# A graph-network kernel whose scatters each get a permission of their own, and a different order of its first steps

## The chip, the cores and the metric

The kernel runs as one program on one core of a Trainium2 chip. A core has a matrix engine (TensorE, PE in the profile, with its weight loads as PEld), a vector engine (VectorE, DVE), a scalar engine (ScalarE, ACT), a general engine (GpSimd, POOL), and a sync engine (SyncE, SP) that here only issues DMAs. Each engine runs its own list of instructions in order, and they meet through semaphores. The metric is the time of one execution on the device, in microseconds.

## The reference

One layer of message passing on a graph with N = 12500 nodes of 128 features and E = 412500 edges with 20 edge features each. Edges are sorted by `dst`; `src` is in no order.

```python
h0  = relu(layernorm(x))                          # 12500 x 128
h   = h0 @ W_in2f                                 # one row a node
Wij = ssp(f @ W_f1 + b_f1) @ W_f2 + b_f2          # one row an edge, from 20 features
Wij = Wij * rcut[:, None]                         # ssp(x) = softplus(x) - log 2
agg = segment_sum(h[dst] * Wij, src, N)           # sum over the edges of a node
out = x + ssp(agg @ W_o1 + b_o1) @ W_o2 + b_o2
```

## The kernel before

**Chunks and steps.** The edges are cut into 806 chunks of 512 (`NCH`), a chunk into four tiles of 128 (`QT`). A long Python loop writes the program out step by step; `step(k)` puts the work for chunk k and for chunks some steps ahead into the engines' lists, and this order is the order in which each engine runs it. In the steady part a step holds:

- `message(k)`: VectorE multiplies the edge's filter row by the row of h that it needs, o = v * hg (L864), and chunk k is put on the list `waiting` of chunks to be scattered.
- `picked` for chunk k+1: ScalarE scales the picked rows of h by `rcut`, four times, into `hg` (L856).
- `value` for chunk k+1: TensorE multiplies the softplus outputs by W_f2 onto a bias that ScalarE wrote earlier, eight matmuls (L834). The last one is kept as `kept["v"]`.
- `pick` for chunk k+2: TensorE takes rows of h from a small window `near` with a one-hot matrix `at` (L846).
- `window`, `end`, `blocks`, `compare`: VectorE's comparisons and the end of softplus for later chunks (L742, L747, L932).
- `rank` and `rank_end` for chunk k+6: two matmuls (L799 `rest_of`, L766 `after`) keep count of how many edges each block of 128 nodes has had, and VectorE's reduction (L771) reads from that the place at which each edge's row will be stored.
- `hidden` for chunk k+4, for two chunks at a time: z = f @ W_f1 (L710), with the exponential and the logarithm on ScalarE in between (L719 to L722).
- `add`: TensorE sums rows of an earlier part of the edges, one unit (L953).

**Scatter and sums.** The products o are not summed at once. Each tile of 128 rows is written by an indirect DMA to a table `slots` in device memory, into a slot of the block that its `src` lies in. These 3224 scatters (four a chunk, L873) all sit in GpSimd's queue. The edges form seven segments (`SEGS`); segment 0 is chunks 0 to 351. When a segment is complete, its table is read back block by block and summed by matmuls with one-hot matrices, beside the chunks of the next segment. These sums begin `DELAY` = 17 steps after the end of a segment, so the first begin in step 369, and they go on until the end.

**What a scatter waits for.** The tile of o (VectorE) and the DMA that used the same of eight semaphores before (the eighth scatter back). Beside these there is an added wait, which orders nothing that the data need: from chunk 24 (`PACED`) until shortly before the end, the first of the four scatters of chunk k-1 (`LAG` = 1) waits for the last v matmul of step k. So GpSimd cannot run ahead of TensorE's step. TensorE in its turn waits in `behind` for the scatters of chunk k-16 (`BACK`), as o has 16 buffers.

**The start.** The nodes come in quads of 512. `make_h` is a generator that makes h for one quad in pieces: load x, layer-norm statistics on VectorE, normalisation, transposes (L367) on TensorE, product with W_in2f (L373), splitting into three bf16 parts, stores to the tables that `near` is loaded from. The first quad, `h[0]`, is done ahead of step -3. The second, `h[1]`, is advanced by one piece within step 0 and by one after each step from 0 on. `HEAD` = (0, 2, 4) are steps whose log and end of softplus stand in other places than usual. For `0 <= k < HEAD[-1]`, that is in steps 0 to 3, the message of chunk k+1 comes in step k, ahead of its counts, and not at the head of step k+1.

Of the kernel before, what the change touches and what calls it, by code (L numbers as in the profile page):

```python
# [17 lines left out]
P = 128  # L18
# [3 lines left out]
QT = CH // P  # L22
# [23 lines left out]
def gnn_kernel(  # L46
# [20 lines left out]
    nc = tc.nc  # L67
# [477 lines left out]
    with tc.tile_pool(name="edge", bufs=2) as edge, tc.tile_pool(  # L545
# [49 lines left out]
        def behind(inst, k, i):  # L595

            if k - BACK >= 0:
                tc.add_manual_dep(inst.ins, puts[(k - BACK) * QT + i],
                                  mybir.DependencyInfo(mybir.DependencyClass.Sync,
                                                       mybir.DependencyReason.DATA),  # L600
                                  reason="pace of the scatters")

        class Group:
# [101 lines left out]
            def hidden(self, c):  # L705

                z = psum.tile([P, 2, CH], F32, name="z")
                for k in range(2):
                    rows = slice(32 * (c + k), 32 * (c + k) + RBF)
                    mm = nc.tensor.matmul(z[:, k, :], wf1[rows, :], self.f[rows, :],  # L710
                                          start=True, stop=True)
                    if k == 1:
                        behind(mm, self.g * NCHUNK + c - LZ, 3)
                self.pair[c] = z

            def hidden_log(self, c):
# [36 lines left out]
            def rank(self, c):  # L753

                seg = self.seg
                if c == 0:
                    self.top = edge.tile([P, TG], F32, name="top")
                    self.slot = edge.tile([P, TG], I32, name="slot", bufs=8)
                k = self.g * NCHUNK + c
                if k > seg.c0:  # L760
                    self.pass_on()
                if k == seg.cleared and k > seg.c0:
                    used = self.used()
                    self.limit(6 * len(segs), ALU.is_gt, seg.low, used[:, :, :NBLK - 1])
                    self.limit(6 * len(segs) + 1, ALU.is_gt, seg.low_last, used[:, :, NBLK - 1:])
                nc.tensor.matmul(free, after, self.inb[c], start=k == seg.c0, stop=False,  # L766
                                 skip_group_check=True)
                kept["inb"] = self.inb[c]

            def rank_end(self, c):  # L770
# [58 lines left out]
            def value(self, c, v):  # L829

                r = self.pair[c // 2 * 2][:, c % 2, :]
                k = self.g * NCHUNK + c - 1
                for i in range(QT):
                    mm = nc.tensor.matmul(v[:, i, :], r[:, i * P:(i + 1) * P], wf2,  # L834
                                          start=False, stop=True, skip_group_check=True)
                    if i == 1:
                        behind(mm, k, k % 2)
                kept["v"] = mm
                return v

            def pick(self, c, at, ps):

                near = self.near.pop(c)
                k = self.g * NCHUNK + c - 2
                for i in range(QT):
                    mm = nc.tensor.matmul(ps[:, i, :], at[:, i * P:(i + 1) * P], near,  # L846
                                          start=i == 0, stop=i == QT - 1, skip_group_check=True)
                    if i == 1:
                        behind(mm, k, 2 + k % 2)

            def picked(self, c, ps):

# [11 lines left out]
                nc.vector.tensor_mul(o[:, :, :P], v, hg)  # L864
                self.o[c] = o

            def scatter(self, c, after=None):

                views = self.seg.views
                o = self.o.pop(c)  # L870
                for i in range(QT):
                    j = c * QT + i
                    put = nc.gpsimd.indirect_dma_start(  # L873
                        out=views[j % VIEWS],
                        out_offset=bass.IndirectOffsetOnAxis(ap=self.slot[:, j:j + 1], axis=0),
                        in_=o[:, i, :],
                        in_offset=None,
                    )
                    puts.append(put.ins.name)
                    if i == 0 and after is not None:  # L880
                        tc.add_manual_dep(
                            put.ins, after.ins.name,
                            mybir.DependencyInfo(mybir.DependencyClass.Sync,
                                                 mybir.DependencyReason.DATA),
                            reason="pace of TensorE")
                    if i == 0 and self.g * NCHUNK + c == self.seg.cleared:
                        for name in self.seg.clears:
                            tc.add_manual_dep(
                                put.ins, name,
                                mybir.DependencyInfo(mybir.DependencyClass.Sync,  # L890
                                                     mybir.DependencyReason.DATA),
                                reason="cleared slots")

        class Collect:
# [47 lines left out]
            def add(self, u):  # L942
                b0, nb, t0, nt = self.units[u]
                m, to = self.m.pop(u), self.to.pop(u)
                for j in range(nb * nt):
                    b, t = b0 + j // nt, t0 + j % nt
                    if b % QT == 0 and t == 0:
                        self.few = QT if "rest" in kept else 2
                    few = self.few
                    i = b % few  # L950
                    if i == 0 and t == 0:
                        self.acc[b // few] = self.room(b // few)
                    nc.tensor.matmul(self.acc[b // few][:, i, :], m[:, j, :P], to[:, j, :],  # L953
                                     start=t == 0, stop=t == self.seg.tiles(b) - 1)
                    if t == self.seg.tiles(b) - 1 and (i == few - 1 or b == NBLK - 1):
                        self.done.append((b, few))
                        owed.append(self)
# [39 lines left out]
        def of(k):  # L997
            return groups[k // NCHUNK], k % NCHUNK
# [14 lines left out]
        def pairs(make):  # L1013
            return lambda g, c: None if c % 2 else make(g, c)
# [34 lines left out]
        tops, ps = [], {}  # L1049
        waiting = []  # L1050
        LAG, PACED = 1, 24

        def step(k, units=()):

# [11 lines left out]
            def message(k):  # L1066
                g, c = of(k)
                g.message(c, vs.pop(k), hgs.pop(k))
                waiting.append(k)
                scatter(k)  # L1070

            def scatter(k, after=None):
                while waiting and (waiting[0] < PACED or k >= NCH - PACED // 2
                                   or after is not None and waiting[0] <= k - LAG):
                    j = waiting.pop(0)
                    g, c = of(j)
                    g.scatter(c, after if j >= PACED and k < NCH - PACED // 2 else None)

            if k in vs:
                message(k)  # L1080
            if not k:
                next(h[1])
            for r in tops:
                for _ in r:
                    pass
# [8 lines left out]
            if has(k + 1):  # L1094
                g, c = of(k + 1)
                hgs[k + 1] = g.picked(c, ps.pop(k + 1))
                if k + 1 not in vs:
                    vs[k + 1] = g.value(c, bs.pop(k + 1))
                    scatter(k, kept["v"])
            if k in HEAD:  # L1100
                part("log", k + LZ - 1, pairs(hidden_log))
            if has(k + 2):
                g, c = of(k + 2)
                if k + 2 not in ps:
                    ps[k + 2] = psum.tile([P, QT, P], F32, name="picked", tag="v", bufs=3)
                g.pick(c, ats.pop(k + 2), ps[k + 2])
                if k + 2 > 0:
                    bs[k + 2] = g.bias(c)
            part("window", k + 3, window)
            if k not in HEAD:  # L1110
                part("end", min(k + LZ - 2, made.get("log", -1)), pairs(hidden_end))
# [4 lines left out]
                    keep()  # L1116
            if k < NCH:
                keep()
            if 0 <= k < HEAD[-1]:
                message(k + 1)  # L1120
            upto = max(made["rank"], min(k + LR, 2 * k + 3))
            ready = [ranks(j) for j in range(made["rank"] + 1, upto + 1)]
# [4 lines left out]
            for r in ready[-1:]:  # L1127
                next(r, None)
                tops.append(r)
            if k in HEAD:  # L1130
                part("end", made["log"] - 1, pairs(hidden_end))
            elif k != -1:
                part("log", min(k + LZ - 1, made["hidden"]), pairs(hidden_log))
            if k not in HEAD[:-1]:
                part("hidden", k + LZ, pairs(hidden))
            for c, u in units:
                if summed:
                    summed[0].add(summed[1])
                summed[:] = c, u

        zeros = {}
        units = {}
# [129 lines left out]
        with tc.manual_schedule():  # L1272
# [36 lines left out]
            for k in range(-3, max(NCH, max(units) + 1)):  # L1309
# [9 lines left out]
                step(k, now)  # L1319

                if k >= 0:
                    for m in h:
                        next(m, None)
                if k > NEXT - 3:
                    next(aside, None)
# [124 lines left out]
```

## Time and profile before

| | |
|---|---|
| time, median of 3 runs | 5023.69 us (5019.35 to 5025.19) |
| profiled execution, its own time | 5066.41 us |
| its span from the first instruction to the last | 5064.7 us |
| mean granted TensorE clock | 0.784 of full speed |
| busy: TensorE matmul, weight load | 3601.4 us (71%), 2760.7 us (55%) |
| busy: VectorE, ScalarE, GpSimd | 3149.0 us (62%), 2793.9 us (55%), 3135.5 us (62%) |
| DMA | 858.10 MB, 169 GB/s on the mean |

How to read the lines that follow. In the table of stretches a row gives the stretch's start and end, its length, and for each engine the busy microseconds and, in brackets, the number of instructions; then the granted clock (PEclk), the share of DMA time and the rate. In the groups, a row reads: line, engine, operation, output <- inputs, x count, then busy time and the mean nanoseconds of one, then the engine's idle time just before these instructions and what ended it. A line of the waits gives the waiting group, what it waited for, the total idle time and how often. In a timeline, a row gives the start, the duration, engine, line, operation, and in square brackets the idle time ahead with the instruction that ended it; "issue" means that the profile shows nothing that it waited for.

### The profile page before, as it was taken

Reading aid. Unit: us, or ns where it says so; the run is one execution under the profiler, and the core shown is the slowest. Engines: PE = TensorE matmul, PEld = TensorE weight load, DVE = VectorE, ACT = ScalarE, POOL = GpSimd, SP = SyncE. Lnnn points to the kernel's source line nnn. Section 1 sums busy time; section 2 is a strip of 40 time slices with the busy share of each in tenths; the row PEclk is TensorE's granted clock in tenths of the full one; section 3 lists DMA queues with packets and bytes.
Section 4 is the critical chain, followed back from the end, with each engine's and each line's share of the span. In section 5 each row is a group of like instructions: output and inputs, shape, how many; then the busy total and the mean of one; then the engine's idle time right before and its main releaser. Section 6 shows DMA issues by size and latency. Waiting matters only on the chain. (4 is left out here: it accounts for less than half of the span.)

```text
span 5064.7 us, 68387 instructions
## 1 busy us (share of the span) xinstructions
PE 3601.4 (71%) x21594; PEld 2760.7 (55%) x21594; DVE 3149.0 (62%) x7192; ACT 2793.9 (55%) x5494; POOL 3135.5 (62%) x3298
## 2 busy tenths in 40 slices
PE   5666666566655565567777887887777787787778
PEld 3444444344433344356666666666666666666667
DVE  5565555555544454556666666666666676677767
ACT  5556566565555555555555555555555555555533
POOL 5566666666666666666666666666656666666553
PEclk7666666766666666679999888888988888888889
DMA  4555545445433334446657655567656765665658
GB/s 140 171 160 164 171 138 174 147 134 160 130 99 114 113 113 141 131 154 199 190 189 238 187 178 185 175 192 230 188 169 185 219 207 168 183 216 163 186 144 229
DMA packets 494767, 858.10 MB, mean 169 GB/s; under 512 B 141018, under 2 KB 276558, under 8 KB 494398
## 3 DMA queue, kind: packets, MB, share of 16 engines
q1 hardware_dynamic: 390798, 640.38, 42.3%
q0 software_dynamic: 103168, 213.15, 12.5%
q8 instruction: 174, 2.85, 0.2%
q14 instruction: 195, 1.60, 0.1%
q10 hardware_dynamic: 432, 0.13, 0.0%
HBM read 457.62 MB, written 395.69 MB: 168 GB/s over the span
## 5 line engine op out<-in xcount | busy, mean ns | idle before, releaser
L873 POOL DMA_INDIRECT slots<-o,slot x3224 | 3090.8, 959 | 1831.2 <-issue 808.9
L856 ACT ACTIVATE hg<-picked,rcut 128x128 f32<-128x128 f32 x3224 | 913.3, 366 | 1243.5 <-remote 356.7
L834 PEld LDWEIGHTS v<-wf,r 128*128 128x128 f32 x6448 | 1067.2, 247 | 324.2 <-issue 214.8
L834 PE MATMUL v<-wf,r 128*128 128x128 f32 x6448 | 1153.8, 335 | 73.4 <-issue 36.5
L864 DVE TENSOR_TENSOR o<-v,hg 128x512 f32<-128x512 f32 x806 | 553.0, 686 | 698.4 <-remote 207.0
L953 PEld LDWEIGHTS acc<-to,m 128*128 128x128 f32 x5660 | 782.1, 219 | 281.0 <-issue 144.0
L953 PE MATMUL acc<-to,m 128*128 128x128 f32 x5660 | 836.6, 308 | 117.1 <-DVE agg L987 45.2
L710 PE MATMUL z<-f,wf 20*128 20x512 f32 x1612 | 605.7, 826 | 355.7 <-issue 185.6
L771 DVE TENSOR_REDUCE top<-free 128x4 f32<-128x392 f32 x806 | 449.1, 557 | 602.2 <-remote 341.9
L932 DVE TENSOR_TENSOR to<-numbers,m 128x640 f32<-128x640 f32 (+3 forms) x793 | 630.4, 825 | 40.0 <-remote 12.0
L719 ACT ACTIVATE a<-z,bf 128x1024 f32<-128x1024 f32 x402 | 445.7, 1109 | 379.4 <-PE v L834 113.6
L747 DVE TENSOR_TENSOR inb<-numbers,blk 128x392 f16<-128x392 f32 x806 | 447.7, 556 | 297.3 <-PE picked L846 73.9
L846 PE MATMUL picked<-near,at 126*128 126x128 bf16 x3224 | 393.6, 248 | 330.2 <-issue 193.5
L799 PE MATMUL free<-inb,rest_of 128*128 128x392 f16 x806 | 318.1, 395 | 420.9 <-issue 277.2
L742 DVE SCALAR_TENSOR_TENSOR r<-z,nbf,a 128x1024 f32<-128x1024 f32 x402 | 513.5, 1277 | 127.9 <-ACT a L722 64.0
L826 ACT ACTIVATE v<-bf 128x512 f32<-128x512 f32 x806 | 486.6, 604 | 180.7 <-DVE o L864 72.5
L846 PEld LDWEIGHTS <-at 126*128 126x128 bf16 x3224 | 302.7, 114 | 389.7 <-issue 364.5
L953 PE MATMUL numbers<-to,m 128*128 128x128 f32 x2492 | 398.7, 324 | 121.0 <-DVE to L932 87.6
L953 PEld LDWEIGHTS numbers<-to,m 128*128 128x128 f32 x2492 | 367.5, 233 | 213.6 <-DVE to L932 136.6
L722 ACT ACTIVATE a<-a,half 128x1024 f32<-128x1024 f32 x402 | 461.5, 1148 | 13.1
L710 PEld LDWEIGHTS z<-f,wf 20*128 20x128 f32 x1612 | 152.4, 226 | 551.7 <-issue 303.0
L720 ACT ACTIVATE a<-a 128x1024 f32<-128x1024 f32 x402 | 424.9, 1057 | 12.8
(126 smaller groups left out, 1845.0 us busy)
## 6 DMA issues: line engine op xcount, KB each, us to landing
m<-slots SPq DMA_DIRECT2D x307, 387.0 KB
rel<-rel_d SPq DMA_DIRECT2D x202, 504.0 KB
m<-slots SPq DMA_DIRECT2D x278, 322.5 KB
f<-in_f_t SPq DMA_DIRECT2D x101, 512.0 KB
slots<-o,slot POOLq DMA_INDIRECT x3224
m<-slots SPq DMA_DIRECT2D x193, 258.0 KB
slots<-zero SPq DMA_DIRECT2D x96, 387.0 KB
slots<-zero SPq DMA_DIRECT2D x58, 516.0 KB
```

The source lines that it names most:

```text
L710: mm = nc.tensor.matmul(z[:, k, :], wf1[rows, :], self.f[rows, :], start=True, stop=True)
L722: nc.scalar.activation(a, a, AF.Ln, bias=half, scale=0.5)
L742: nc.vector.scalar_tensor_tensor(r, z, nbf1, a, op0=ALU.max, op1=ALU.add)
L771: nc.vector.tensor_reduce(self.top[:, c * QT:(c + 1) * QT], free_v, axis=mybir.AxisListType.X, op=ALU.max)
L826: nc.scalar.activation(v, spread(bf12, QT), AF.Copy)
L834: mm = nc.tensor.matmul(v[:, i, :], r[:, i * P:(i + 1) * P], wf2, start=False, stop=True, skip_group_check=True)
L846: mm = nc.tensor.matmul(ps[:, i, :], at[:, i * P:(i + 1) * P], near, start=i == 0, stop=i == QT - 1, skip_group_check=True)
L856: nc.scalar.activation(hg[:, i, :], ps[:, i, :], AF.Copy, scale=self.rcut[:, j:j + 1])
L864: nc.vector.tensor_mul(o[:, :, :P], v, hg)
L873: put = nc.gpsimd.indirect_dma_start(out=views[j % VIEWS], out_offset=bass.IndirectOffsetOnAxis(ap=self.slot[:, j:j + 1], axis=0), in_=o[: ...
L932: nc.vector.tensor_tensor(to[:, :n, :], count_ps[:, None, :].to_broadcast([P, n, P]), m[:, :n, P:].to_broadcast([P, n, P]), op=ALU.is_equal)
L953: nc.tensor.matmul(self.acc[b // few][:, i, :], m[:, j, :P], to[:, j, :], start=t == 0, stop=t == self.seg.tiles(b) - 1)
```

## The change

It has two parts.

**Scatters from chunk 369 on** (`LONE = segs[0].c1 + DELAY`, the step in which the sums begin). The single name `kept["v"]` becomes `kept["mm"]`, the last matmul written so far, and is set by `hidden`, `rank`, `value`, `pick` and `add`. `scatter` is called at four points of a step: after v, after pick, after the counts and at the end of the step. For chunks 24 to 368 it acts at the first point alone, as before. For later chunks each point lets one scatter go, and that one waits for the last matmul ahead of the point. The four scatters of chunk k-1 are still those of step k.

**The first steps.** `h[1]` stays where it is until after step 6; its six pieces come in steps 6 to 11. In steps 1 and 3 the hidden matmuls of chunk k+4 and the v matmuls of chunk k+2 come ahead of the counts. The message of chunk 5 comes in step 4.

```diff
@@ hidden, rank (L766), pick, add: the same assignment in each
-                nc.tensor.matmul(free, after, self.inb[c], start=k == seg.c0, stop=False,
-                                 skip_group_check=True)
+                kept["mm"] = nc.tensor.matmul(free, after, self.inb[c], start=k == seg.c0,
+                                              stop=False, skip_group_check=True)
@@ value
-                kept["v"] = mm
+                kept["mm"] = mm
@@ scatter of a segment
-            def scatter(self, c, after=None):
+            def scatter(self, c, tiles, after=None):
                 views = self.seg.views
-                o = self.o.pop(c)
-                for i in range(QT):
+                o = self.o[c] if tiles[-1] < QT - 1 else self.o.pop(c)
+                for i in tiles:
...
-                    if i == 0 and after is not None:
+                    if i == tiles[0] and after is not None:
@@ step
+        LONE = segs[0].c1 + DELAY
...
-                waiting.append(k)
+                waiting.append((k, 0))
                 scatter(k)
 
-            def scatter(k, after=None):
-                while waiting and (waiting[0] < PACED or k >= NCH - PACED // 2
-                                   or after is not None and waiting[0] <= k - LAG):
-                    j = waiting.pop(0)
-                    g, c = of(j)
-                    g.scatter(c, after if j >= PACED and k < NCH - PACED // 2 else None)
+            def scatter(k, point=None):
+                while waiting:
+                    j, i = waiting[0]
+                    if j < PACED or k >= NCH - PACED // 2:
+                        n, after = QT - i, None
+                    else:
+                        where, n = ("v", QT) if j < LONE else ("each", 1)
+                        if point not in (("v", "pick", "rank", "end") if where == "each" else (where,)):
+                            return
+                        if j * QT + i + n > (k - LAG + 1) * QT:
+                            return
+                        after = kept["mm"]
+                    while n > 0:
+                        j, i = waiting.pop(0)
+                        g, c = of(j)
+                        e = min(QT, i + n)
+                        g.scatter(c, range(i, e), after)
+                        after = None
+                        n -= e - i
+                    if e < QT:
+                        waiting.insert(0, (j, e))
+                        return
...
-            if not k:
-                next(h[1])
...
-                    scatter(k, kept["v"])
+                    scatter(k, "v")
...
                 g.pick(c, ats.pop(k + 2), ps[k + 2])
+                scatter(k, "pick")
                 if k + 2 > 0:
                     bs[k + 2] = g.bias(c)
+                if k in (1, 3):
+                    part("hidden", k + LZ, pairs(hidden))
+                    vs[k + 2] = g.value(c, bs.pop(k + 2))
...
-            if 0 <= k < HEAD[-1]:
+            if 0 <= k <= HEAD[-1]:
                 message(k + 1)
...
                 tops.append(r)
+            scatter(k, "rank")
...
                 summed[:] = c, u
+            scatter(k, "end")
...
                 if k >= 0:
-                    for m in h:
+                    for m in h[:1] if k <= HEAD[-1] + 1 else h:
                         next(m, None)
```

GpSimd's list at one chunk of segment 1 and the first scatter of the next, before. A row is a scatter; in brackets are the semaphores that it waits for: DMASW0 to DMASW7 are the eight of the earlier scatters, DVE is the tile o, PE is TensorE.

```order
L873 DMA slots_117<-o,slot 116992x129 [waits DMASW0_49,DVE_49,PE_49]
L873 DMA slots_117<-o,slot 116992x129 [waits DMASW1_49]
L873 DMA slots_117<-o,slot 116992x129 [waits DMASW2_49]
L873 DMA slots_117<-o,slot 116992x129 [waits DMASW3_49]
L873 DMA slots_117<-o,slot 116992x129 [waits DMASW4_49,DVE_49,PE_49]
```

The same place after the change:

```order
L875 DMA slots_117<-o,slot 116992x129 [waits DMASW0_49,DVE_49,PE_49]
L875 DMA slots_117<-o,slot 116992x129 [waits DMASW1_49,PE_49]
L875 DMA slots_117<-o,slot 116992x129 [waits DMASW2_49,PE_49]
L875 DMA slots_117<-o,slot 116992x129 [waits DMASW3_49,PE_49]
L875 DMA slots_117<-o,slot 116992x129 [waits DMASW4_49,DVE_49,PE_49]
```

The scatters stand in the same order and number; each of the second, third and fourth has a wait on TensorE that it did not have.

TensorE's list from the end of step 1 into step 2, before. `free` is the count, `z` the hidden layer, `xps` the transposes of the second quad, `v` the filter rows.

```order
L799 LDWEIGHTS rest_of
L799 MATMUL free<-inb,rest_of 128x392
L766 LDWEIGHTS after
L766 MATMUL free<-inb,after 128x392
L799 LDWEIGHTS rest_of
L799 MATMUL free<-inb,rest_of 128x392
L766 LDWEIGHTS after
L766 MATMUL free<-inb,after 128x392
L710 MATMUL z<-f,wf_62 128x512 x2
L367 MATMUL xps<-ident,xb 128x128 x4
L834 MATMUL v<-wf_63,r 128x128 x4
```

The same place after the change, where lines below L711 have moved by one (L800 is L799 of before, L767 is L766, L835 is L834):

```order
L710 MATMUL z<-f,wf_62 128x512 x2
L835 MATMUL v<-wf_63,r 128x128 x4
L800 LDWEIGHTS rest_of
L800 MATMUL free<-inb,rest_of 128x392
L767 LDWEIGHTS after
L767 MATMUL free<-inb,after 128x392
L800 LDWEIGHTS rest_of
L800 MATMUL free<-inb,rest_of 128x392
L767 LDWEIGHTS after
L767 MATMUL free<-inb,after 128x392
```

z and the v of an odd chunk went ahead of the two pairs of counts, and the transposes are gone from this place; they stand some seven steps later.

More of the change, by code (lines that the diff above doesn't have):

```diff
@@ L837, in value @@
                         behind(mm, k, k % 2)
-                kept["v"] = mm
+                kept["mm"] = mm
                 return v
@@ L849, in pick @@
                         behind(mm, k, 2 + k % 2)
+                kept["mm"] = mm
             def picked(self, c, ps):
@@ L952, in add @@
                         self.acc[b // few] = self.room(b // few)
-                    nc.tensor.matmul(self.acc[b // few][:, i, :], m[:, j, :P], to[:, j, :],
-                                     start=t == 0, stop=t == self.seg.tiles(b) - 1)
+                    kept["mm"] = nc.tensor.matmul(
+                        self.acc[b // few][:, i, :], m[:, j, :P], to[:, j, :],
+                        start=t == 0, stop=t == self.seg.tiles(b) - 1)
                     if t == self.seg.tiles(b) - 1 and (i == few - 1 or b == NBLK - 1):
```

## The prediction

> **What bounds the kernel now.** I read the page first (no engine is busy for more than 71% of the span), then the table of busy time by stretch for the two long stages, chunks 24 to 351 and chunks 369 to 793.
>
> ```profile
> span 5064.7 us, 68387 instructions
> PE 3601.4 (71%) x21594; PEld 2760.7 (55%) x21594; DVE 3149.0 (62%) x7192; ACT 2793.9 (55%) x5494; POOL 3135.5 (62%) x3298
> core 0: us, PE busy (x) PEld busy (x) DVE busy (x) ACT busy (x) POOL busy (x), PEclk, DMA share, GB/s
> 186.00:2122.00 1936.00, 1172.84 (x5508) 793.74 (x5507) 1040.90 (x2664) 1130.64 (x2239) 1258.31 (x1312) 0.66 0.45 141
> 2220.00:4844.00 2624.00, 2074.27 (x14004) 1691.29 (x14002) 1795.20 (x3801) 1423.05 (x2801) 1628.98 (x1700) 0.87 0.62 192
> ```
>
> The second stretch is the one that the change is about: 1700 scatters are 425 chunks, so a chunk takes 2624 / 425 = 6.17 us. The groups of instructions by line, for GpSimd in that stretch, split this time:
>
> ```profile
> L873 POOL DMA_INDIRECT slots<-o,slot x1700 | 1629.0, 958 | 994.9 <-issue 415.6 <-PE free L766 199.7 <-PE picked L846 164.5
> POOL slots L873 <- issue: 415.6, 1354, 1.2
> ```
>
> A scatter is 0.958 us, and the gap that nothing explains is 415.6 / 1354 = 0.307 us; so one costs 1.265 us and a chunk 5.06. The second line is of the view of waits (us in total, times, longest). Of the 994.9 us idle, 1700 x 0.307 = 522 are this gap; the other 473 us are true stops, 1.11 us a chunk. The stage is therefore a row of scatters at GpSimd's own rate, plus stops. What ends a stop shows in GpSimd's timeline:
>
> ```profile
> 2691.12 0.96 POOL L873 DMA_INDIRECT slots<-o,slot  x1 [1.21 <-PE free L766]
> 2692.39 0.95 POOL L873 DMA_INDIRECT slots<-o,slot  x1 [0.30 <-issue]
> ...
> 2697.73 0.96 POOL L873 DMA_INDIRECT slots<-o,slot  x1 [1.86 <-PE free L766]
> ...
> 2702.78 0.96 POOL L873 DMA_INDIRECT slots<-o,slot  x1 [0.31 <-issue]
> ...
> 2709.71 0.96 POOL L873 DMA_INDIRECT slots<-o,slot  x1 [2.19 <-PE free L766]
> ...
> 2721.68 0.95 POOL L873 DMA_INDIRECT slots<-o,slot  x1 [2.18 <-PE free L766]
> ```
>
> The left-out rows all have a gap of 0.30 or 0.31. Runs are four scatters long (2691.12 to 2697.73) or eight (2697.73 to 2709.71, and again to 2721.68), and each ends with GpSimd waiting for the v matmul of a step. Less the 0.30, a stop is 0.91 or 1.56 us after four and 1.89 or 1.88 after eight. TensorE's and VectorE's timelines at the third stop show why:
>
> ```profile
> 2705.10 1.06 PE L834 MATMUL v<-wf,r 128*128 128x128 f32 x8
> 2705.99 0.56 PE L846 MATMUL picked<-near,at 126*128 126x128 bf16 x4
> 2707.76 0.33 PE L799 MATMUL free<-inb,rest_of 128*128 128x392 f16 x1 [1.21 <-issue]
> 2709.18 0.33 PE L766 MATMUL free<-inb,after 128*128 128x392 f16 x1 [1.09 <-issue]
> 2709.54 0.69 DVE L864 TENSOR_TENSOR o<-v,hg 128x512 f32<-128x512 f32 x1 [3.17 <-PE free L766]
> ```
>
> The v that the scatter at 2709.71 waits for was through by 2705.10 + 1.06 = 2706.16, yet both VectorE's o and the scatter go on only at 2709.54 and 2709.71, some 3.5 us later and 2 us after GpSimd fell idle (at 2707.8). TensorE's signals leave late while GpSimd issues scatters, and they come together, v, pick and count at once, soon after it stops. So a stop is a handshake: GpSimd must run out of permission before TensorE can give it more.
>
> **The change part by part.** *The scatters from chunk 369 on.* Before, a chunk's four wait for one point, its step's last v matmul. Now the first waits for v, the second for pick, the third for the count matmul (L766), the fourth for the step's last matmul (sums or z). Queued behind a waiting scatter on GpSimd are only later scatters; o has 16 buffers and TensorE's own wait on scatters is 16 chunks back, so nobody waits for a scatter that is a microsecond late. The cover is those 16 chunks, about 99 us.
>
> What three more waits a chunk cost as such: the row at 2702.78 is a chunk's first scatter, with waits on a lane, on VectorE and on TensorE, and its gap is 0.31 like those without, so I put the issue cost at nothing. [...]
>
> What the finer waits do to the stops is the term that matters, and the trace of before has no scatter that waits for pick, count or sums alone. Bounds from the rows: below, every chunk costs the short stop of 0.91 us, 425 x 0.91 = 387, that is 86 less than 473. Above, a second stop of 0.91 us in every chunk, 387 more. The rows place the truth near the middle of the lower part. At 2709.71 the signals came together, so a run of four or eight is let through as before. In a run of four the sums' signal stands one place ahead of v in TensorE's order, so the fourth scatter gets off about when GpSimd would otherwise have stopped; stops then come after three or five scatters and are of the short kind. I take half of the lower bound: -43 us.
>
> *The second quad of nodes.* Its pieces leave steps 0 to 5 for steps 6 to 11. In the old place:
>
> ```profile
> 22.82 0.28 DVE L346 BATCH_NORM_STATS2 st<-xb 128x6 f32<-128x128 f32 x1
> ...
> 24.32 0.18 DVE L347 BATCH_NORM_AGGREGATE mv<-st 128x2 f32<-128x6 f32 x1
> 24.54 0.30 ACT L350 ACTIVATE rs<-mv,eps 128x4 f32<-128x4 f32 x1 [1.73 <-DVE mv L347]
> 38.60 1.12 PE L367 MATMUL xps<-ident,xb 128*128 128x128 f32 x4
> 43.77 1.35 PE L373 MATMUL hps<-win,xT 128*128 128x128 f32 x8
> 35.60 0.96 POOL L873 DMA_INDIRECT slots<-o,slot  x1 [2.38 <-DVE o L864]
> 42.50 0.96 POOL L873 DMA_INDIRECT slots<-o,slot  x1 [2.16 <-DVE o L864]
> 49.23 0.95 POOL L873 DMA_INDIRECT slots<-o,slot  x1 [1.99 <-DVE o L864]
> 57.83 0.96 POOL L873 DMA_INDIRECT slots<-o,slot  x1 [3.86 <-DVE o L864]
> ```
>
> Eight statistics take VectorE from 22.82 to 24.50 and hold ScalarE (1.73 us idle) ahead of hg; the transposes and products take TensorE 1.12 and 1.35 us ahead of a v. GpSimd waits for o meanwhile: the four stops, less 0.30 each, are 9.2 us, and that bounds what steps 0 to 5 can give back. The same pieces then stand in steps 6 to 11, where they can take back as much. Its stores pass SP's queue in step 11 instead of 4, behind the loads of near, which run six steps ahead, some 37 us. *z and odd chunks' v ahead of the counts, and chunk 5's o one step earlier* belong to the same 9.2 us. Between -9 and +9 I take -3, as the first steps wait for o in every chunk.
>
> *Sum.* -43 - 3 = -46 us on the profiled execution's 5066.4 (span 5064.7, 1.7 outside), so 5020. It ran 0.85% longer than the median of 5023.69. I carry the difference over one to one: 5024 - 46 = 4978. With this case's own ends, -86 - 9 and -10, it is 4929 to 5014.
>
> **The rivals.** *A second stop* (slower). The fourth scatter now starts at the step's last matmul, and v follows that directly on TensorE (2705.10 is the row after the sums). Its 1.27 us of issuing thus fall on the time in which v, pick and count want to signal; those that ScalarE and VectorE wait for leave late, and GpSimd, after one scatter, stops again for at least 0.91 us. It decides from 43 / 0.91 = 47 chunks of 425 on, one in nine. In one chunk of three it is 142 x 0.91 = 129, less 43: +86, 5110 us; in all chunks, 387 with nothing gained, 5411. For it speaks that every signal in the 2705 to 2709 rows that meets a running GpSimd is late; against it, that they came together and so would pass the whole chunk. Chance 0.28.
>
> *The stops only move* (no change). If the signals of v, pick, count and sums always come out together, four waits open at the moment one did: 5024 within 10 us. In effect the change then does not do what it says. For it speaks that stops after four and after eight cost nearly the same by the chunk, 0.91 against 1.89 / 2 = 0.94. Chance 0.14.
>
> *The clock falls* (slower). Granted clock was 0.87 in this stretch and 0.66 in the one before, where TensorE is busy 61% of the time against 79%. If pauses of TensorE were spread so that it fell half way, to 0.765, its 2074 us would become 2359; of these 285 us between none and all reach the end. A third gives 5024 + 95 = 5119. [...] Against it, TensorE does not wait for scatters here. Chance 0.05.
>
> *The handshake is gone* (much faster). If short pauses let every signal out, half of 473 goes: 5024 - 237 = 4787. Against it, the shortest stop quoted is 0.91. Chance 0.05.
>
> **How the numbers follow.** The forecast case has 0.48. About 0.2% (10 us) is what a measurement of this kernel can tell from no change. Faster by more than that: 0.48 + 0.05 = 0.53; within it: 0.14; slower: 0.28 + 0.05 = 0.33. The range runs from 4890 (stops at 0.80 us a chunk, beyond the case's own 4929, since half a bound was a choice) to 5110 (a second stop in one chunk of three). Outside lie the vanished handshake and the worse halves of the two slow cases, 0.05 + 0.14 at most.
>
> **What would show it.** Right: in the stretch of chunks 369 to 793 the idle of GpSimd before scatters falls from 995 us to about 950, the stops of 2.2 us become rare, runs of three and five stand beside those of four, and the scatters' own 0.958 us stays. The first scatters after 35 us come some 2 us earlier for each step and lose most of that by chunk 12. Wrong: stops in front of the fourth scatter and again in front of the first, with an idle total well over 995; or a granted clock under 0.87; or scatter gaps of over 0.31 within a run, which would be the price of the waits themselves.

## The result and the profile after

The changed kernel takes 4996.33 us in the median of 5 runs (4986.01 to 5006.41), the kernel before 5023.69 (5019.35 to 5032.80): a ratio of 0.9945, 95% interval 0.9927 to 0.9964, or 27 us less (18 to 37). The forecast was 4978, 46 us less, in a range from 4890 to 5110.

The profiled execution of the changed kernel has a span of 5004.7 us. The page's head:

```profile
span 5004.7 us, 69659 instructions
PE 3584.2 (72%) x21594; PEld 2750.6 (55%) x21594; DVE 3153.7 (63%) x7192; ACT 2790.5 (56%) x5494; POOL 3146.1 (63%) x3298
```

The table of stretches, chunks 24 to 351 and then the 1700 scatters of chunks 369 to 793, after the change:

```profile
184.20:2095.90 1911.70, 1165.60 (x5506) 791.53 (x5504) 1040.11 (x2666) 1131.62 (x2241) 1262.52 (x1313) 0.66 0.46 143
2194.90:4774.30 2579.40, 2068.00 (x14059) 1690.13 (x14058) 1806.50 (x3813) 1422.75 (x2809) 1634.68 (x1700) 0.88 0.64 195
```

Both stretches are shorter than in the profile that the prediction read: the second by 45 us (2624 before), close to the forecast term of 43, and the first by 24 (1936 before), though nothing was changed in it. Two profiles of different kernels cannot say how much of that is the change's. So the kernel before was profiled a second time (first experiment below), in an execution near its median; its two stretches:

```profile
183.00:2091.80 1908.80, 1176.45 (x5517) 794.78 (x5514) 1042.86 (x2669) 1133.67 (x2245) 1262.57 (x1313) 0.66 0.46 143
2190.60:4789.80 2599.20, 2083.18 (x14055) 1702.49 (x14051) 1796.27 (x3810) 1429.74 (x2808) 1635.80 (x1700) 0.87 0.63 194
```

Against this one, chunks 24 to 351 are the same within 3 us, and chunks 369 to 793 are 19.8 us shorter. The first profile was of an execution that was long in both stretches. The scatters of the second stretch in the groups by line, of the second profile of before and of the changed kernel:

```profile
L873 POOL DMA_INDIRECT slots<-o,slot x1700 | 1635.8, 962 | 963.4 <-issue 418.7 <-PE free L766 171.4 <-PE picked L846 139.1
```

```profile
L875 POOL DMA_INDIRECT slots<-o,slot x1700 | 1634.7, 962 | 944.8 <-issue 378.2 <-PE acc L955 125.2 <-PE numbers L955 96.9
```

Scatters cost the same (962 ns); GpSimd's idle time ahead of them fell from 963 to 945 us. The stops, counted in GpSimd's timeline as gaps of over 0.49 us, less the usual 0.30, were 268 of 1.66 us on the mean before (446 us) and are 344 of 1.24 us now (427 us). These 19 us account for the difference between the two profiled executions (5024.86 and 5006.41 us); the changed one was the longest of its five, and the medians differ by 27. The releasers moved too: count and pick (L766, L846) led before, the sums (L955, `acc` and `numbers`), whose last matmul ends a step, lead now. A releaser is the matmul that had ended last when TensorE's signal came, not always the one waited for: before, every first scatter waited for v (L834). "Remote" means that the trace finds none. GpSimd's timeline at chunks 451 to 453 shows the new place:

```profile
2684.61 0.96 POOL L875 DMA_INDIRECT slots<-o,slot  x1 [0.31 <-issue]
2685.88 0.96 POOL L875 DMA_INDIRECT slots<-o,slot  x1 [0.30 <-issue]
2687.14 0.96 POOL L875 DMA_INDIRECT slots<-o,slot  x1 [0.30 <-remote]
2690.17 0.96 POOL L875 DMA_INDIRECT slots<-o,slot  x1 [2.07 <-PE v L835]
2691.43 0.96 POOL L875 DMA_INDIRECT slots<-o,slot  x1 [0.30 <-issue]
2692.70 0.96 POOL L875 DMA_INDIRECT slots<-o,slot  x1 [0.30 <-issue]
2693.97 0.96 POOL L875 DMA_INDIRECT slots<-o,slot  x1 [0.31 <-issue]
2695.24 0.96 POOL L875 DMA_INDIRECT slots<-o,slot  x1 [0.30 <-PE v L835]
2696.50 0.96 POOL L875 DMA_INDIRECT slots<-o,slot  x1 [0.30 <-issue]
2699.41 0.98 POOL L875 DMA_INDIRECT slots<-o,slot  x1 [1.95 <-PE acc L955]
```

2684.61 is the first scatter of chunk 451, and the one at 2690.17 its fourth: the stop is within the chunk, before the scatter that waits for the end of the step. The one at 2699.41 is the second of chunk 453. Of the 344 stops, 200 stand before a fourth scatter (1.46 us on the mean), 108 before a first (0.94), 36 before the second or third.

### The profile page after: what moved, and what is told of

The parts are those of the page before. It is cut to its first block, busy times and chain, and to the rows that moved or that the text cites. A ratio compares the mean times of both kernels' runs of the same rounds, so it can differ in the third digit from the quotient of the medians.

```text
span 5004.7 us, 69659 instructions
## 1 busy us (share of the span) xinstructions
PE 3584.2 (72%) x21594; PEld 2750.6 (55%) x21594; DVE 3153.7 (63%) x7192; ACT 2790.5 (56%) x5494; POOL 3146.1 (63%) x3298
## 5 line engine op out<-in xcount | busy, mean ns | idle before, releaser
L835 PEld LDWEIGHTS v<-wf,r 128*128 128x128 f32 x6448 | 1054.4, 243 | 336.9 <-issue 209.5
L835 PE MATMUL v<-wf,r 128*128 128x128 f32 x6448 | 1148.0, 332 | 84.9 <-issue 40.6
L955 PEld LDWEIGHTS acc<-to,m 128*128 128x128 f32 x5660 | 774.4, 217 | 278.7 <-issue 148.6
L955 PE MATMUL acc<-to,m 128*128 128x128 f32 x5660 | 825.0, 306 | 118.7 <-DVE agg L990 44.8
L800 PE MATMUL free<-inb,rest_of 128*128 128x392 f16 x806 | 320.3, 397 | 317.4 <-issue 215.7
L955 PEld LDWEIGHTS numbers<-to,m 128*128 128x128 f32 x2492 | 377.2, 238 | 205.5 <-DVE to L934 106.4
L955 PE MATMUL numbers<-to,m 128*128 128x128 f32 x2492 | 407.8, 330 | 112.7 <-DVE to L934 60.9
```

Of the source, the lines that this page charges most:

```text
L955: kept["mm"] = nc.tensor.matmul(self.acc[b // few][:, i, :], m[:, j, :P], to[:, j, :], start=t == 0, stop=t == self.seg.tiles(b) - 1)
```

## The experiments

Two theories stood against each other. **A**: the finer waits in chunks 369 to 793 shorten GpSimd's stops, and that is the whole change. **B**: the new first steps set the phase in which GpSimd follows, and chunks 24 to 351 gain by it.

**The kernel before, a second profile.**

> The kernel before once more, for a second profile. If the stretches repeat, chunks 24 to 351 take 1936 us and chunks 369 to 793 2624 us within 5 us, and the difference of 25 us in chunks 24 to 351 belongs to the change (theory B). If they scatter by 20 us or more between two profiles of one kernel, that difference is none of the change's (theory A), and the profiled execution's excess of 41 us over the median lies there.

5024.86 us in one execution; chunks 24 to 351 take 1908.8 us and chunks 369 to 793 2599.2, as shown above. Two profiles of one kernel differ by 27 and 25 us in these stretches, so the 24 us in chunks 24 to 351 cannot be put down to the change. B loses its ground.

**The scatters' part alone**: the first steps are put back.

```diff
+            if not k:
+                next(h[1])
...
-                if k in (1, 3):
-                    part("hidden", k + LZ, pairs(hidden))
-                    vs[k + 2] = g.value(c, bs.pop(k + 2))
...
-            if 0 <= k <= HEAD[-1]:
+            if 0 <= k < HEAD[-1]:
...
-                    for m in h[:1] if k <= HEAD[-1] + 1 else h:
+                    for m in h:
```

> The scatters of chunk 369 on each have a wait of their own; the first steps are those of before. Theory A (the finer waits shorten GpSimd's stops in chunks 369 to 793, 477 us of them before and 427 after): this alone gives most of the change, 4993 to 5003 us; true stops in that stretch 420 to 435 us, with runs of 1 to 8 scatters. Theory B (the new first steps set the phase in which GpSimd follows the others, and chunks 24 to 351 go faster by it: 1936 us in the profile before, 1912 after): this alone keeps only a part, 5005 to 5015 us, and chunks 24 to 351 take 1936 us again.

5001.26 us, a ratio of 0.9948 (0.9935 to 0.9962), beside a median of 5028.04 for the kernel before: the whole change within its interval. Stops in chunks 369 to 793 are 430 us. Chunks 24 to 351 take 1908 us with the old first steps, where theory B wanted 1936 again.

**The first steps' part alone**: the scatters' waits are put back.

```diff
-        LONE = segs[0].c1 + DELAY
+        LONE = NCH
```

> The new first steps alone; every scatter's waits are those of before. Theory A: 5015 to 5025 us, chunks 369 to 793 take 2610 to 2625 us in the profile, in runs of four and eight scatters. Theory B: 4998 to 5010 us, with chunks 24 to 351 at about 1912 us.

5021.87 us, 0.9993 (0.9981 to 1.0005): no change that can be told. The stops in chunks 369 to 793 are 446 us, those of before, in runs of four and eight; the stretch takes 2593.7 us, less than A expected, since that expectation still went by the first profile of before. Chunk 12's first scatter comes at 101.4 us, where it came at 102.8 and 102.7 in the two profiles of before; in the changed kernel's profile chunk 24's come at 184.2 us, in the two of before at 185.8 and 183.1, so by then the lead is within what two profiles differ by. Chunk 12's lead says little as well: with the old first steps (the run before this one) it came at 100.1 us.

**As many waits, nearly one place**: the four scatters wait for the four quarters of v.

```diff
-                        if point not in (("v", "pick", "rank", "end") if where == "each" else (where,)):
+                        if point not in (("v0", "v1", "v2", "v3") if where == "each" else (where,)):
...
+                    for i, mm in enumerate(kept["quarters"]):
+                        kept["mm"] = mm
+                        scatter(k, f"v{i}")
```

> As the change, but the four scatters from chunk 369 on wait for four neighbouring matmuls, the quarters of v, within about 1 us: as many waits, nearly one place. Theory A (what counts is that permission comes at four points spread over the step): the gain is gone, 5012 to 5028 us, runs of four and eight in chunks 369 to 793, true stops 460 to 490 us. Rival C (any wait of its own breaks up the run and lets TensorE's signals out, wherever it lies): as the change, 4990 to 5003 us. [...]

The edit does a second thing. A matmul that a scatter waits for has to signal, and the first three quarters of v did not: TensorE's signalling matmuls in chunks 369 to 793 rise from 2380 in the changed kernel to 3647.

5041.39 us, 1.0035 (1.0021 to 1.0049): the gain is gone, and it is 13 us slower than before's median of 5028.04 beside it. The scatters' row of chunks 369 to 793:

```profile
L878 POOL DMA_INDIRECT slots<-o,slot x1700 | 1634.7, 962 | 985.8 <-issue 348.6 <-PE v L836 245.1 <-PE picked L850 168.7
```

Idle is 986 us, 22 more than in the second profile of before, and the stops are 468 us; 273 of the 283 stops stand before a first scatter again, and the runs are of four (124) and eight (139). So a wait of its own does not break up a run wherever it lies (rival C falls). A gap within a run is 0.30 us here too, so waits as such have no price that shows. That it came out slower than before was expected by neither theory A nor rival C. The 1267 added signals may be the reason, and may also have eaten a part of a gain; no run has the one without the other, so how much is due to the place alone stays open here.

**No wait for TensorE at all** from chunk 369 on.

```diff
-                    if j < PACED or k >= NCH - PACED // 2:
+                    if j < PACED or j >= LONE or k >= NCH - PACED // 2:
```

> Again no wait on TensorE from chunk 369 on. Where the kernel before takes about 4200 us (no stops, scatters in a row from chunk 24 on) it is within 0.1 per cent of before, as it was. Where before takes about 5025 us: theory A says that a wait for TensorE at the right place is what keeps stops short, so without it GpSimd stops only for o, late and long: 5040 to 5120 us. Rival E (waits are pure loss): 4900 us or less.

5163.90 us, 1.0269 (1.0247 to 1.0292), where before takes 5029.48. The scatters' row of chunks 369 to 793:

```profile
L875 POOL DMA_INDIRECT slots<-o,slot x1700 | 1634.6, 962 | 1102.9 <-DVE o L866 612.9 <-issue 451.2 <-DVE at L819 18.6
```

GpSimd now waits for VectorE's o, 2.13 us in each of 274 stops, 585 us in all. Taking the waits away makes the stops longer, because o itself is late: in these chunks VectorE stood idle ahead of o for 394 us although v and hg had both been written, against 206 us in the second profile of before. So theory A's direction holds, and the price was larger than its 5120. That a wait on TensorE helps as a pause given early is the reading that fits; it is not shown by itself.

**Three scatters with v, one at the end of the step.**

```diff
-                        where, n = ("v", QT) if j < LONE else ("each", 1)
-                        if point not in (("v", "pick", "rank", "end") if where == "each" else (where,)):
+                        where, n = ("v", QT) if j < LONE else ("each", 3 if point == "v" else 1)
+                        if point not in (("v", "end") if where == "each" else (where,)):
```

> Once more: three scatters go with v, the fourth with the last matmul of the step, from chunk 369 on. Where the kernel before takes about 5025 us: theory A1 (the step's end is the point that does it) ratio 0.993 to 0.997, with stops before the first and the fourth scatter alone and 420 to 435 us of them; rival A4 (each of the four places earns its part) 0.997 to 1.000, stops 435 to 450 us. Where before takes about 4200 us: no difference, which says nothing between the two.

4998.48 us, 0.9945 (0.9925 to 0.9964), where before takes 5025.00: the same ratio as the whole change. GpSimd's scatters, and two of its stops, which stand before the fourth scatters of chunks 447 and 449:

```profile
L875 POOL DMA_INDIRECT slots<-o,slot x1701 | 1630.4, 959 | 946.9 <-issue 403.4 <-PE picked L847 109.7 <-PE acc L955 83.6
```

```profile
2677.22 0.95 POOL L875 DMA_INDIRECT slots<-o,slot  x1 [2.08 <-PE picked L847]
2678.48 0.96 POOL L875 DMA_INDIRECT slots<-o,slot  x1 [0.30 <-issue]
...
2689.13 0.95 POOL L875 DMA_INDIRECT slots<-o,slot  x1 [2.12 <-PE picked L847]
```

Idle is 947 us as in the changed kernel (945), stops are 428 us, 218 before a fourth scatter, 94 before a first and none elsewhere. So the one wait at the end of the step is enough, and the waits for pick and count add nothing that these intervals show; A4's 0.997 or more lies outside (A1 against A4). Whether one wait after pick or after the counts would do as much was not run where signals are late.

**The same kernels on other chips.** The experiments above ran on three chips, where the kernel before takes 5025 to 5029 us. Two groups of runs fell on two other chips, and there it takes 4202 or 4209 us. The edits: the one just shown (twice), the one without waits, two scatters at v and two at the end of the step, and the change's four waits from chunk 24 on (twice).

```diff
+                        where, n = ("v", QT) if j < LONE else ("each", 2)
+                        if point not in (("v", "end") if where == "each" else (where,)):
...
+        LONE = PACED
```

> As the change, but only the fourth scatter of a chunk waits for a place of its own, the last matmul of the step; the first three go with v. In the changed kernel's profile 199 of 344 stops in chunks 369 to 793 stand before the fourth scatter and 108 before the first, 36 before the other two. Theory A1 (the step's end is the point that does it): as the change, 4993 to 5005 us, stops 420 to 435 us. Rival A4 (each of the four quarters earns its part): half of the gain, 5008 to 5018 us, stops 435 to 450.

> As the change, but two scatters go with v and two with the last matmul of the step. Theory A1: 4990 to 5008 us. Rival A4: 5000 to 5015 us, since two points do part of what four do. If a run that is cut in the middle costs two stops in most chunks (the prediction's second stop), 5050 us or more.

> The change's four waits from chunk 24 on, not 369. In chunks 24 to 351 a step holds no sums, so rank and the step's end are next to each other every other step; stops are 246 to 278 us there, mostly 2.1 us after twelve scatters. If finer waits shorten stops in that stage as in the later one, 4 per cent of them: 10 us less, 4980 to 4992 us. If cutting a run of twelve only brings more stops (three of about 1 us in place of one of 2.1), 246 becomes 330 us or more and the time 5070 to 5100 us.

> From chunk 369 on no scatter waits for TensorE at all: it goes as soon as its o is written. Theory A (a stop is what lets TensorE's signals out, so the place of the wait sets how often and how long): without a wait GpSimd still stops, for o, as o itself waits for late signals; stops of the long kind, 500 us or more in chunks 369 to 793, 5040 to 5120 us. Rival E (the waits are pure loss; GpSimd's rate of 5.06 us a chunk is all that counts): 4700 to 4900 us.

> Again: three scatters go with v, the fourth with the last matmul of the step, from chunk 369 on. Where the kernel before takes about 5025 us: theory A1 (the step's end is the point that does it; 199 of the changed kernel's 344 stops stand there) gives the whole change, ratio 0.993 to 0.997; rival A4 (each of the four places earns its part) half of it or less, 0.997 to 1.000.

> Again: the change's four waits from chunk 24 on. Where the kernel before takes about 5025 us: if finer waits shorten stops in chunks 24 to 351 too (246 to 278 us of them there), ratio 0.990 to 0.994; if cutting runs of twelve scatters only brings more stops, three of about 1 us in place of one of 2.1, they grow to 330 us or more and the ratio is 1.008 or more.

The times are 4200.83, 4199.07, 4199.84 and 4200.49 beside 4202.33 of before, and 4206.51 and 4206.86 beside 4208.91: ratios from 0.9993 to 0.9995, each with 1 inside its interval. The four times expected on the first of these chips were for a kernel of 5025 us, and none was near; the last two expectations hold for such a kernel alone. What is different shows in the kernel without waits, on the chip of the 4202 us, in the stretch, the scatters' row and three engines' timelines:

```profile
1898.10:4047.50 2149.40, 1861.96 (x14000) 1549.67 (x13999) 1778.78 (x3796) 1401.98 (x2781) 1631.03 (x1700) 0.93 0.76 232
```

```profile
L875 POOL DMA_INDIRECT slots<-o,slot x1700 | 1631.0, 959 | 518.3 <-issue 400.6 <-DMA slots<-o,slot 39.0 <-DVE o L865 20.1
```

```profile
2703.61 0.96 POOL L875 DMA_INDIRECT slots<-o,slot  x1 [0.30 <-issue]
2703.39 0.39 PE L847 MATMUL picked<-near,at 126*128 126x128 bf16 x4
2703.82 1.14 ACT L858 ACTIVATE hg<-picked,rcut 128x128 f32<-128x128 f32 x4 [0.53 <-PE picked L847]
```

There is no stop: 518.3 us of idle are 1700 gaps of 0.305. The pick is through by 2703.78, and ScalarE starts on it at 2703.82, in the midst of a scatter. In the prediction's rows, from a chip of the other kind, v was through by 2706.16, and VectorE, idle for 3.17 us, went on with o only at 2709.54, once GpSimd had stopped:

```profile
2709.54 0.69 DVE L864 TENSOR_TENSOR o<-v,hg 128x512 f32<-128x512 f32 x1 [3.17 <-PE free L766]
```

Over chunks 369 to 793 VectorE stood idle ahead of o, with v and hg both written, for 220 us in that profile of before, up to 4.4 us at a time, and for 2.9 us here, never over 0.3.

So where TensorE's signals are not held up, GpSimd's own rate of 5.06 us a chunk bounds both stages (2149.4 us for 425 chunks, 1660 for the 328 of chunks 24 to 351), and no permission matters. These runs say nothing on pairs of scatters or on the four waits from chunk 24 on where signals are late; both are open.

## Why the prediction was right, and where its size was off

*Direction and range.* Faster, and inside the range. The forecast was 46 us and the change is 27 (18 to 37).

*The bound.* Stops of GpSimd in chunks 369 to 793, ended by late signals of TensorE: shown. The chip without late signals has no stops (518.3 us of idle in 1700 gaps of 0.305), and where signals are late the stops without the waits are longer (2.13 us on the mean, 1.66 in the second profile of before). The first trace of before also holds the moments at which TensorE's semaphore stepped up: in these chunks 1273 of the 2086 recorded steps fall into GpSimd's stops, which are 22% of the time, although only 514 of the 2374 matmuls that signal end there. It does not show whether GpSimd's scatters hold the signals up or something that goes with them.

*The scatters' term, -43.* Right in kind: stops after three scatters (33) and five (74) are new and short, 0.84 and 0.96 us on the mean, and idle times of 2 us or more fell from 136 in the second profile of before to 48. The size is wrong: stops fell by 19 us (446 to 427), not by 43, and the scatters' part alone is worth 0.9948 of the time, 26 us. The step that was off is the bound of 387 us and "I take half of the lower bound". Two things went into it.

- The price of a short stop, 0.91 us, was one row. In the same profile the 160 stops after four scatters are 1.34 us on the mean and the 131 after eight 1.99. At 1.34 us, one stop in every chunk would be 570 us, more than there was. In the changed kernel stops after four (87) still cost 1.29 us, and those after seven and eight (92) 1.72 and 1.79.
- The 473 us were one profile's. By the prediction's own working the second profile has 963.4 - 522 = 441 us, 54 over the bound of 387, and half of that is 27. That this would have met the measured 27 is luck, as neither the 0.91 nor the half came out of the runs.

The idle of "about 950" was met in the same way: it is 945, but the second profile of before, with nothing changed, has 963 and not 995.

*"In a run of four the sums' signal stands one place ahead of v in TensorE's order, so the fourth scatter gets off about when GpSimd would otherwise have stopped."* The place was right, and stops after three and five followed. But the fourth scatter does not mostly get off: 200 of the 344 stops stand right before it, 1.46 us on the mean. The three-and-one run shows that its wait is what helps; why a pause there is the cheaper one is argued and not shown.

*What three more waits cost.* Nothing, as taken. The row to read, the third scatter of a chunk in the changed kernel, which now waits for TensorE:

```profile
2670.09 0.96 POOL L875 DMA_INDIRECT slots<-o,slot  x1 [0.30 <-PE numbers L955]
```

The gap of 0.30 us with one more wait is the gap without it, so the trace shows no price of the wait here. Over all scatters of chunks 369 to 793 that follow without a stop, the mean gap is 0.305 us before and 0.306 after.

*The first steps, -3.* The first steps alone gave 0.9993 (0.9981 to 1.0005), 3.5 us less, which can't be told from nothing. The sign that was to show it did not come either: chunk 2's first scatter is 2.2 us earlier than before, but chunk 3's 1.8 us later and chunk 4's 0.3.

*The rivals.* The second stop (0.28) has its place right and its sum wrong: 47 of 425 chunks have two stops or more, just the number from which it was to decide, yet the total fell. "The stops only move" (0.14) is refuted by 0.9945, but the stops did mostly move: of 446 us, 427 are left. The clock did not fall (0.87 and 0.88 in the stretch). The chance left outside the range was summed a little low: half of 0.28 and of 0.05 is 0.165, not 0.14. The handshake that vanishes altogether (0.05) did not come from this change; other chips have it so.

## What to carry to other kernels

When one engine's signals are held up while another works, ask where the pause comes, not how many waits there are: one more wait at the end of the step gave the whole gain, four at nearly one place gave none (with more signals to send, too), and without any it was 2.7% slower. Before sizing a term from one profiled execution, see how far its stretches stand from the median; here a second profile of the same kernel moved them by 25 and 27 us, as much as the whole change. And take the price of a wait from all of its rows, not from one.

## What the hardware did that was not expected

Chips differ. The same program takes 5025 to 5029 us on three and 4202 or 4209 us on two others, 16% less. On a faster one TensorE's signals reach the others while GpSimd issues scatters (0.04 us from the end of a pick to ScalarE); on the slower ones many come late (3.4 us from the end of v to o in the stop shown).

Two more things differ in the traces. In chunks 369 to 793 TensorE itself stood idle for 284 to 334 us on the slower chips, in gaps that nothing in the trace ends (both profiles of before, the changed kernel, the one without waits), and never so in the kernel without waits on a faster chip. And of VectorE's 6529 signals the first trace of before holds 3034, that of the changed kernel 3019 of 6530, that faster one 6507 of 6530. So in the traces of the slower kind the recording, too, loses what it should hold; whether it has a part in the delay no run here shows, and nothing says what else differs in the chips. An order of waits that is worth 0.55% on the one kind is worth nothing on the other.
